# Layer norms applied by ScalarE, and softmax and gamma products held in PSUM, in a four-layer graph network kernel

## The chip, the cores and the metric

The kernel runs on one core of a Trainium2 chip. The metric is the device time of one execution in microseconds (us); the time before is the median of three runs. The engines are called as in the profile: PE (TensorE, matrix products), DVE (VectorE), ACT (ScalarE), POOL (GpSimd) and SP (SyncE, which issues the DMAs). PE reads SBUF and writes PSUM[...].

## The reference, cut to what matters

The input x is 128 graphs of 64 nodes with 512 features, 8192 rows in all. Four layers each end in `x = layernorm(x + layer(x))`.

```python
def _layernorm(x, axis=-1, eps=1e-5):
    m, v = mean(x), var(x)
    return (x - m) / sqrt(v + eps)

x = _layernorm(x + L0(x))     # deg * (x @ Wi.T + b) + adj @ (x @ Wj.T)
x = _layernorm(x + L1(x))     # four attention heads over the 64 nodes, elu, an output head, elu,
                              # feed-forward, and an inner layer norm times gamma plus beta
x = _layernorm(x + L2(x))     # one attention head
x = _layernorm(x + L3(x))     # one attention head
```

An attention is `softmax(where(adj > 0, leaky_relu(f1[:, None] + f2[None, :]), fill))` over 64 neighbours, times the projected rows. Everything is float32.

## The kernel before, in words

The 8192 rows are worked in 32 blocks of two tiles (t = 0, 1) of 128 rows; a tile holds two graphs. A block p goes through stages, each a Python generator: `stage_first` (layer 0), `stage_scores` (attention scores, softmax and aggregation of the four heads), `stage_heads` and `stage_project` (the heads' weights and the output projection), `stage_out` (output head, feed-forward, inner layer norm) and `stage_gat` twice (layers 2 and 3). Large products use seven block products in place of eight (`seven` and `strassen`); their partial sums lie in two PSUM tiles, `stx` and `sty`, which ACT or DVE adds into SBUF piece by piece.

No engine instruction is issued where it is written. `Plan` records each call as a step, and `Plan.order` (line 207) lists the steps by assumed costs (`cost`, line 319), by readiness, by free buffers and by rank; `play` then issues them. So every engine's order comes from the planner, a new step on one engine can shift the order on all of them, and every instruction of the recorded program has line 306 in the profile. `with nc.soon()` lowers the rank of steps by 1000, so that they go ahead of others that are ready. Engines work in order: an instruction that waits holds up all behind it. PSUM is one pool of eight tiles with tag `b`; a step that opens a tile waits until one of the eight is free.

The names that matter below:

- `moments(x, name)`, line 688: `bn_stats` and `bn_aggr` on DVE give mean and variance (`st`, `mv`); two tiny POOL instructions make `rs` = (variance + eps) ** -0.5.
- `normalize(x, name)`, line 699: `moments`, then one DVE instruction over the 128 x 512 tile in SBUF (`x<-x,mv,rs`). It is called for each tile after each of the four layers, 256 times.
- `attention_heads`, line 714: once for each block. PE multiplies `dg` with a block matrix into the PSUM tile `bc`; DVE adds `f` into the SBUF tile `e` (128 x 512: two tiles by four heads by 64 neighbours), then applies the leaky slope, the mask, the maximum, the subtraction; ACT takes the exponential; DVE sums, inverts, and multiplies. PE then transposes `e` into `pt`; ACT copies it to `aT`; `yp` are the products with it.
- `norms(t)` in `stage_out`, line 1053: the inner layer norm. One DVE instruction forms (o - mean) * gamma in SBUF (`o<-o,mv_1i,rows_gamma`), a second multiplies by `rs_1i` and adds x (`x<-o,rs_1i,x`); then `normalize`. 64 times.
- `dots` makes attention scores `f` on DVE (custom instruction, `j<-x,rows`); in the first microseconds the same instruction makes score weights `wa_h` (`j_h`). For blocks 0 and 1, PE makes the scores (`fp`) from transposed rows (`x1Tp`, `x1T`) and `wa_h`.
- For the first four blocks, layer 0 is done plainly: `l` are its products on PE.

Of the kernel before, what the change touches and what calls it, by code (L numbers as in the profile page):

```python
# [12 lines left out]
FP = mybir.dt.float32  # L13
BF = mybir.dt.bfloat16
I32 = mybir.dt.int32
AF = mybir.ActivationFunctionType
ALU = mybir.AluOpType
AX = mybir.AxisListType
PSUM = bass.MemoryType.PSUM

P = 128
# [318 lines left out]
def gnn_stack_kernel(  # L340
# [24 lines left out]
    nc = Plan(tc)  # L365
    NT, D = x.shape
# [13 lines left out]
    small = nc.pool(ctx, name="small", bufs=4)  # L380

    psum = nc.pool(ctx, name="ps", bufs=8, space=PSUM)
# [16 lines left out]
    def rows(srcs, name, tag="rows"):  # L399

        bufs = {"rows": 2, "A": NA}.get(tag, 1)
        t = unit.tile([P, 2, D], FP, tag=tag, bufs=bufs, name=f"rows_{name}")
        for i, src in enumerate(srcs):
            nc.sync.dma_start(out=t[:, i, :], in_=src.partition_broadcast(P))
        return t
# [26 lines left out]
    fill1 = cp.tile([P, 1], FP, tag="fill1", name="fill1")  # L432
# [9 lines left out]
    mask1 = cp.tile([P, N], I32, tag="mask1", name="mask1")  # L442
# [132 lines left out]
    def part_from(name, p, K=D):  # L575

        ring, bufs = RINGS[K]

        def part(q):
            t = unit.tile([P, K // P, D // 2], FP, tag=ring, bufs=bufs, name=f"ws_{name}_{p}_{q}")  # L580
            nc.sync.dma_start(out=t, in_=streams[name][q])
            return t
        return part
# [104 lines left out]
    def moments(x, name):  # L688

        stats = small.tile([P, 6], FP, tag="stats", name=f"st_{name}")  # L690
        mv = small.tile([P, 2], FP, tag="mv", name=f"mv_{name}")
        nc.vector.bn_stats(stats, x)
        nc.vector.bn_aggr(mv, stats)
        rstd = small.tile([P, 1], FP, tag="rstd", name=f"rs_{name}")
        nc.gpsimd.tensor_scalar(rstd, mv[:, 1:2], EPS, None, ALU.add)
        nc.gpsimd.tensor_tensor(rstd, rstd, mhalf, ALU.pow)
        return mv[:, 0:1], rstd

    def normalize(x, name):

        mean, rstd = moments(x, name)
        nc.vector.tensor_scalar(x, x, mean, rstd, ALU.subtract, ALU.mult)

    def dots(f, x, rows, name):

# [8 lines left out]
    def attention_heads(f, name):  # L714

        bc3 = [P, G, N]

        dg = unit.tile([P, G, N], FP, tag="dg", name=f"dg_{name}")
        nc.vector.tensor_tensor(
            dg,  # L720
            f[:, 1, :].unsqueeze(2).to_broadcast(bc3),
            ident2.unsqueeze(1).to_broadcast(bc3),
            ALU.mult,
        )
        yield 2.0
        ps = psum.tile([P, G, N], FP, tag="b", name=f"bc_{name}")
        nc.tensor.matmul(ps, lhsT=bones, rhs=dg, start=True, stop=True)
        e = unit.tile([P, G, N], FP, tag="e", name=f"e_{name}")
        nc.vector.tensor_tensor(e, ps, f[:, 0, :].unsqueeze(2).to_broadcast(bc3), ALU.add)
        nc.vector.scalar_tensor_tensor(e, e, 0.01, e, ALU.mult, ALU.max)  # L730
        nc.vector.copy_predicated(
            e, mask1.unsqueeze(1).to_broadcast(bc3), fill1.unsqueeze(1).to_broadcast(bc3)
        )
        mx = small.tile([P, G], FP, tag="mx", name=f"mx_{name}")
        nc.vector.tensor_reduce(mx, e, AX.X, ALU.max)
        nc.vector.tensor_tensor(e, e, mx.unsqueeze(2).to_broadcast(bc3), ALU.subtract)
        nc.scalar.activation(e, e, AF.Exp)
        sm = small.tile([P, G], FP, tag="sm", name=f"sm_{name}")
        nc.vector.tensor_reduce(sm, e, AX.X, ALU.add)
        r = small.tile([P, G], FP, tag="r", name=f"r_{name}")  # L740
        nc.vector.reciprocal(r, sm)
        nc.vector.tensor_tensor(e, e, r.unsqueeze(2).to_broadcast(bc3), ALU.mult)
        yield 10.0

        pt = psum.tile([P, G // 2, P], FP, tag="b", name=f"pt_{name}")
        with nc.together():
            for q in range(G // 2):
                nc.tensor.transpose(
                    pt[:, q, :], e[:, 2 * q : 2 * q + 2, :].rearrange("p s j -> p (s j)"), ident
                )  # L750
        aT = unit.tile([P, G // 2, 2, N], FP, tag="aTh", name=f"aT_{name}")
        for b in range(2):
            for s in range(2):
                nc.scalar.copy(aT[ts(b, N), :, s, :], pt[ts(s, N), :, ts(b, N)])
        return aT
# [38 lines left out]
    def elu(dst, ps):  # L794

        with nc.soon():
            nc.scalar.activation(dst, ps, AF.Relu, scale=-1.0)
            nc.scalar.activation(dst, dst, AF.Exp, scale=-1.0)
            nc.vector.scalar_tensor_tensor(dst, dst, -1.0, ps, ALU.add, ALU.max)
# [67 lines left out]
    def stage_scores(p):  # L867
# [23 lines left out]
        for h2 in range(H // 2 if p >= 2 else 0):  # L891
            for s in range(2):
# [5 lines left out]
                )  # L898
        yield 3.0
        aT = yield from attention_heads(f, f"1_{p}")  # L900
        yield 3.0

# [93 lines left out]
    def stage_out(p):  # L996

        while p not in outs:
            yield 1.0
        x = xs[p]  # L1000
        who, f = outs.pop(p)
        pt = yield from attention(
            f, 0.01, mask1, fill1.to_broadcast([P, N]), None, f"1o_{p}"
        )
        aT = unit.tile([P, T, N], FP, tag="aT", bufs=2, name=f"aT_1o_{p}")
        with nc.soon():
            for b in range(2):
                for t in range(T):
                    nc.scalar.copy(aT[ts(b, N), t, :], pt[ts(t, N), ts(b, N)])
        yield 2.0  # L1010
        o = unit.tile([P, T, D], FP, tag="o", name=f"o_{p}")
        oT = unit.tile([P, KC, T * P], FP, tag="A", bufs=NA, name=f"oT_{p}")

        ps = [psum.tile([P, D], FP, tag="b", name=f"op_{p}_{t}") for t in range(T)]
        with nc.together():
            for b in range(2):
                for t in range(T):
                    nc.tensor.matmul(
                        ps[t][ts(b, N), :], lhsT=aT[ts(t, N), b, :], rhs=who[ts(t, N), b, :],
                        start=True, stop=True,  # L1020
                    )
        for t in range(T):
            elu(o[:, t, :], ps[t])
        yield 6.0
        b2_sb = rows([b2], f"b2_{p}")[:, 0, :]
        yield 2.0
        for t in range(T):
            ps = psum.tile([P, KC, P], FP, tag="b", name=f"oTp_{p}_{t}")
            with nc.together():
                for k in range(KC):  # L1030
                    nc.tensor.transpose(ps[:, k, :], o[:, t, ts(k, P)], ident)
            nc.scalar.copy(oT[:, :, ts(t, P)], ps)
            nc.gpsimd.tensor_tensor(o[:, t, :], o[:, t, :], b2_sb, ALU.add)
            yield 2.0
        hid = unit.tile([P, 2, T, KC // 2, P], FP, tag="A", bufs=NA, name=f"hid_{p}")
        for q in range(KC // 2):
            ps = psum.tile([P, 2, T * P], FP, tag="b", name=f"hidp_{p}_{q}")
            for c in range(2):
                with nc.together():
                    for k in range(KC):  # L1040
                        nc.tensor.matmul(
                            ps[:, c, :], lhsT=w1_sb[:, k, ts(2 * q + c, P)], rhs=oT[:, k, :],
                            start=(k == 0), stop=(k == KC - 1),
                        )
            for c in range(2):
                nc.scalar.activation(
                    hid[:, q, :, c, :], ps[:, c, :].rearrange("p (t i) -> p t i", t=T), AF.Relu,
                    bias=b1_sb[:, 2 * q + c : 2 * q + c + 1],
                )
            yield 6.0  # L1050
        gamma_sb = rows([gamma], f"gamma_{p}")[:, 0, :]

        def norms(t):
            ot, xt = o[:, t, :], x[:, t, :]
            mean, rstd = moments(ot, f"1i_{p}_{t}")
            nc.vector.scalar_tensor_tensor(ot, ot, mean, gamma_sb, ALU.subtract, ALU.mult)
            nc.vector.scalar_tensor_tensor(xt, ot, rstd, xt, ALU.mult, ALU.add)
            normalize(xt, f"1_{p}_{t}")

        A = lambda k, t: hid[:, k, t, :, :]  # L1060
        nc.gpsimd.tensor_tensor(A(0, 1), A(0, 1), A(1, 1), ALU.add)
        yield from strassen(
            A, part_from("w2", p, D // 2), sums(A, KC // 2, nc.gpsimd), o, KC // 2, f"y_{p}", 1.8,
            whole=norms,
        )
        yield 4.0
# [150 lines left out]
```

## Time and profile before

| | |
|---|---|
| median of 3 runs | 3404.39 us (3404.05 to 3405.88) |
| profiled execution | 3404.41 us |
| its span, first to last instruction | 3402.6 us |
| PE busy | 3285.9 us (97%) |
| DVE busy | 2655.5 us (78%) |
| POOL busy | 1771.1 us (52%) |
| ACT busy | 1163.7 us (34%) |
| mean granted PE clock | 0.989 |

The profiled execution is 1.8 us longer than its span, and lies on the median. A busy PE is one with matrix products in its pipeline. Rows of groups give the engine, the operation, the tiles written and read, shapes and count, then busy time in us and the mean of one in ns, and then the engine's idle time just before them with what ended it. In rows of waits stand the total, the number of times and the longest wait, in us.

### The profile page before, as it was taken

What the parts mean: (1) busy time and instruction counts of PE and PEld (TensorE: products, weight loads), DVE (VectorE), ACT (ScalarE), POOL (GpSimd) and SP (SyncE); (2) the same over time, 40 slices, a digit from 0 to 9 for tenths busy, and PEclk for the clock granted to TensorE, in tenths of its full rate; (3) what the DMA queues carried; (4) which work ended last, traced back from release to release, by engine and by line L of the source; (5) the groups of instructions that cost most, each with busy time, mean ns of one, the idle gap of its engine ahead of it and who ended that gap; (6) DMA issues with size and microseconds to landing.
All of it is one profiled execution on the core that took longest, in us unless ns stands there. A gap on an engine that the chain in (4) does not pass through costs nothing.

```text
span 3402.6 us, 59449 instructions
## 1 busy us (share of the span) xinstructions
PE 3285.9 (97%) x21300; PEld 2898.4 (85%) x21300; DVE 2655.5 (78%) x5696; ACT 1163.7 (34%) x2924; POOL 1771.1 (52%) x1866
## 2 busy tenths in 40 slices
PE   8799999999999999999999999999999999999986
PEld 4688888888888888988888988888988888888874
DVE  7767777888778878778877787878787887877855
ACT  1333333333333333333333333333333333333321
POOL 6854455554455554455554555554555544555432
PEclk9899999999999999999999999999999999999998
DMA  7766666666666666656666666666666676666643
GB/s 279 273 211 204 195 212 220 216 215 221 201 203 220 219 215 220 205 207 220 216 218 215 204 204 221 222 215 219 203 204 219 216 226 207 202 216 211 202 158 118
DMA packets 302500, 720.42 MB, mean 212 GB/s; under 512 B 32848, under 2 KB 42112, under 8 KB 302208
## 3 DMA queue, kind: packets, MB, share of 16 engines
q1 hardware_dynamic: 302208, 716.63, 64.5%
q8 instruction: 171, 2.80, 0.3%
q14 instruction: 121, 0.99, 0.1%
HBM read 683.18 MB, written 33.32 MB: 211 GB/s over the span
## 4 chain that ended last, share of the span: by engine, by line
PE 76%; DVE 16%; DMA 3%; POOL 3%; issue 2%; SPq 1%; ACT 0%; POOLq 0%; DVEq 0%; ACTq 0%
PE stx_h L306 13%; PE stx L306 11%; PE stx_o L306 11%; PE sty_h L306 10%; PE sty L306 9%; PE hidp L306 6%; PE sty_o L306 5%; DVE e L306 4%; PE gp L306 3%; DVE x L306 3%; DVE o L306 2%; PE stx_y L306 1%; PE yp L306 1%; DVE st_1i L306 1%; PE sty_y L306 1%
## 5 line engine op out<-in xcount | busy, mean ns | idle before, releaser
L306 DVE CUSTOM_DVE_ANT_0 j<-x,rows 128x512 bf16<-128x512 f32 x736 | 636.3, 864 | 51.5 <-DMA rows<-d_h 42.5
L306 PE MATMUL stx_h<-ys,wh 128*128 128x128 f32 x3072 | 402.8, 276 | 8.0 <-DVE hT L306 7.9
L306 PEld LDWEIGHTS stx_h<-ys,wh 128*128 128x128 f32 x3072 | 386.2, 192 | 28.0 <-issue 7.3
L306 ACT COPY hT<-stx_h 128x256 f32<-128x256 f32 x384 | 142.5, 372 | 571.9 <-PE stx_h L306 562.7
L306 POOL TENSOR_SCALAR rs<-mv 128x1 f32<-128x1 f32 x256 | 90.9, 355 | 454.2 <-DVE mv L306 449.8
L306 DVE TENSOR_SCALAR x<-x,mv,rs 128x512 f32<-128x512 f32 x256 | 222.0, 867 | 72.4 <-POOL rs L306 72.1
L306 PE MATMUL sty_h<-ys,wh 128*128 128x128 f32 x2048 | 274.0, 277 | 0.0
L306 PEld LDWEIGHTS sty_h<-ys,wh 128*128 128x128 f32 x2048 | 254.3, 192 | 7.1
L306 PE MATMUL sty_o<-ws_wo,hT 128*128 128x256 f32 x1024 | 242.9, 380 | 2.5 <-DMA ws_wo<-d_wo 1.2
L306 PE MATMUL stx_o<-ws_wo_T,s_o 128*128 128x256 f32 x1024 | 244.3, 381 | 0.2
L306 POOL TENSOR_TENSOR ys<-ys,t 128x256 f32<-128x256 f32 x128 | 111.9, 877 | 252.0 <-PE sty_h L306 251.8
L306 DVE TENSOR_TENSOR x<-stx,x 128x256 f32<-128x256 f32 x368 | 154.3, 419 | 112.8 <-PE stx L306 110.3
L306 PE MATMUL hidp<-oT,w 128*128 128x256 f32 x1024 | 234.8, 379 | 0.7 <-ACT oT L306 0.7
L306 ACT ACTIVATE elu<-hT 128x512 f32<-128x512 f32 x256 | 154.1, 602 | 224.8 <-DVE hT L306 220.3
L306 PEld LDWEIGHTS sty_o<-ws_wo,hT 128*128 128x128 f32 x1024 | 189.5, 190 | 28.5 <-POOL hT L306 3.3
L306 PEld LDWEIGHTS hidp<-oT,w 128*128 128x128 f32 x1024 | 191.5, 190 | 25.4 <-ACT oT L306 0.9
L306 PEld LDWEIGHTS stx_o<-ws_wo_T,s_o 128*128 128x128 f32 x1024 | 187.5, 190 | 24.7 <-POOL hT L306 0.3
L306 DVE SCALAR_TENSOR_TENSOR hT<-elu,hT 128x512 f32<-128x512 f32 x256 | 174.9, 684 | 16.3 <-ACT elu L306 14.7
L306 ACT COPY ys<-yp 128x512 f32<-128x512 f32 x256 | 131.2, 606 | 158.3 <-PE yp L306 147.0
L306 DVE BATCH_NORM_STATS2 st<-x 128x6 f32<-128x512 f32 x256 | 176.3, 689 | 4.8
L306 POOL TENSOR_TENSOR rs<-rs,mhalf 128x1 f32<-128x1 f32 x256 | 162.5, 635 | 21.3
L306 DVE TENSOR_TENSOR x<-sty,x 128x256 f32<-128x256 f32 (+1 forms) x184 | 102.1, 555 | 81.6 <-PE sty L306 81.1
(184 smaller groups left out, 7734.8 us busy)
## 6 DMA issues: line engine op xcount, KB each, us to landing
ws_wo_T<-d_wo_T SPq DMA_DIRECT2D x256, 512.0 KB, 3.8
ws_wo<-d_wo SPq DMA_DIRECT2D x192, 512.0 KB, 4.0
ws_W_T<-d_W_T SPq DMA_DIRECT2D x256, 256.0 KB, 3.3
rows<-d_h SPq DMA_DIRECT2D x240, 256.0 KB, 4.5
ws_w_T<-d_w_T SPq DMA_DIRECT2D x112, 512.0 KB, 4.3
ws_W<-d_W SPq DMA_DIRECT2D x192, 256.0 KB, 3.7
ws_w<-d_w SPq DMA_DIRECT2D x84, 512.0 KB, 3.8
ws_w_T<-d_w_T SPq DMA_DIRECT2D x128, 256.0 KB, 4.8
```

The lines of the kernel that those rows point to most:

```text
L306: getattr(getattr(self.tc.nc, s.engine), name)(*map(real, args), **{k: real(v) for k, v in kw.items()})
```

## The change

Three edits. (1) `normalize` now makes `shift` = -mean * rs, a 128 x 1 value, on DVE, and ACT applies the norm to the tile as Identity(rs * x + shift), in place, with both as values for each partition (a token's row). (2) In `attention_heads` the first addition still goes from `bc` to `e`; the leaky step now writes into the PSUM tile `bc`, where mask, maximum, subtraction, exponential and sum then work, and the last multiplication writes `e` from it. (3) In `norms` the product with gamma goes to a new PSUM tile `ng`, and the second instruction reads it from there; both are recorded under `soon()`.

```diff
     def normalize(x, name):
         mean, rstd = moments(x, name)
-        nc.vector.tensor_scalar(x, x, mean, rstd, ALU.subtract, ALU.mult)
+        shift = small.tile([P, 1], FP, tag="shift", name=f"sh_{name}")
+        nc.vector.scalar_tensor_tensor(shift, mean, -1.0, rstd, ALU.mult, ALU.mult)
+        nc.scalar.activation(x, x, AF.Identity, bias=shift, scale=rstd)
...
         nc.vector.tensor_tensor(e, ps, f[:, 0, :].unsqueeze(2).to_broadcast(bc3), ALU.add)
-        nc.vector.scalar_tensor_tensor(e, e, 0.01, e, ALU.mult, ALU.max)
+        nc.vector.scalar_tensor_tensor(ps, e, 0.01, e, ALU.mult, ALU.max)
         nc.vector.copy_predicated(
-            e, mask1.unsqueeze(1).to_broadcast(bc3), fill1.unsqueeze(1).to_broadcast(bc3)
+            ps, mask1.unsqueeze(1).to_broadcast(bc3), fill1.unsqueeze(1).to_broadcast(bc3)
         )
...
-        nc.vector.tensor_reduce(mx, e, AX.X, ALU.max)
-        nc.vector.tensor_tensor(e, e, mx.unsqueeze(2).to_broadcast(bc3), ALU.subtract)
-        nc.scalar.activation(e, e, AF.Exp)
+        nc.vector.tensor_reduce(mx, ps, AX.X, ALU.max)
+        nc.vector.tensor_tensor(ps, ps, mx.unsqueeze(2).to_broadcast(bc3), ALU.subtract)
+        nc.scalar.activation(ps, ps, AF.Exp)
...
-        nc.vector.tensor_reduce(sm, e, AX.X, ALU.add)
+        nc.vector.tensor_reduce(sm, ps, AX.X, ALU.add)
...
-        nc.vector.tensor_tensor(e, e, r.unsqueeze(2).to_broadcast(bc3), ALU.mult)
+        nc.vector.tensor_tensor(e, ps, r.unsqueeze(2).to_broadcast(bc3), ALU.mult)
...
             mean, rstd = moments(ot, f"1i_{p}_{t}")
-            nc.vector.scalar_tensor_tensor(ot, ot, mean, gamma_sb, ALU.subtract, ALU.mult)
-            nc.vector.scalar_tensor_tensor(xt, ot, rstd, xt, ALU.mult, ALU.add)
+            ps = psum.tile([P, D], FP, tag="b", name=f"ng_{p}_{t}")
+            with nc.soon():
+                nc.vector.scalar_tensor_tensor(ps, ot, mean, gamma_sb, ALU.subtract, ALU.mult)
+                nc.vector.scalar_tensor_tensor(xt, ps, rstd, xt, ALU.mult, ALU.add)
             normalize(xt, f"1_{p}_{t}")
```

## The prediction

> **What bounds the kernel now.** First the page's busy line, then PE's waits, then busy time by stretch (PE, PEld, DVE, ACT, POOL, then PE clock, DMA share, GB/s).
>
> ```profile
> PE 3285.9 (97%) x21300; PEld 2898.4 (85%) x21300; DVE 2655.5 (78%) x5696; ACT 1163.7 (34%) x2924; POOL 1771.1 (52%) x1866
> ```
> ```profile
> PE pt L306 <- DVE e L306: 24.4, 13, 10.5
> PE bc L306 <- DVE f L306: 21.3, 7, 4.2
> PE yp L306 <- DVE who L306: 11.1, 12, 1.3
> PE stx_h L306 <- DVE hT L306: 7.9, 4, 5.1
> ...
> PE gp L306 <- ACT aTg L306: 1.5, 2, 0.7
> ```
> ```profile
> 0.00:100.00 100.00, 76.00 (x312) 40.30 (x312) 73.25 (x128) 13.38 (x28) 70.64 (x66) 0.92 0.82 292
> 100.00:200.00 100.00, 90.27 (x689) 84.38 (x690) 65.99 (x112) 39.91 (x90) 71.17 (x49) 0.93 0.79 268
> ...
> 1500.00:1600.00 100.00, 99.86 (x657) 89.07 (x656) 80.92 (x176) 35.35 (x88) 52.80 (x55) 1.00 0.65 214
> ...
> 3300.00:3400.00 100.00, 62.23 (x267) 49.04 (x267) 59.60 (x153) 16.92 (x58) 28.14 (x44) 0.80 0.34 108
> ```
>
> PE bounds it. All that any edit off PE can win is PE's idle time, 3402.6 - 3285.9 = 117 us: 34 us in the first 200, 38 in the last 100, and in 300 to 3100 only some 30 us of waits, of which DVE ends 22 and ACT none. DVE's 78% is not a bound, so its lightening by itself is worth nothing there.
>
> The groups that the change touches, and prices for what it adds, from the groups of DVE (the second fence with shapes kept apart) and of ACT; the figure after the busy time is the mean of one in ns:
>
> ```profile
> L306 DVE TENSOR_SCALAR x<-x,mv,rs 128x512 f32<-128x512 f32 x256 | 222.0, 867 | 72.4 <-POOL rs L306 72.1
> L306 DVE SCALAR_TENSOR_TENSOR x<-o,rs_1i,x 128x512 f32<-128x512 f32 x64 | 84.0, 1313 | 2.8 <-POOL rs_1i L306 2.4
> L306 DVE TENSOR_TENSOR e<-e,mx 128x512 f32<-128x512 f32 x32 | 39.1, 1221 | 1.1
> L306 DVE TENSOR_SCALAR r<-r,has 128x2 f32<-128x2 f32 x64 | 26.1, 409 | 2.2
> L306 DVE TENSOR_TENSOR x<-l,x 128x512 f32<-128x512 f32 x8 | 5.5, 682 | 0.7 <-PE l L306 0.7
> ```
> ```profile
> L306 DVE TENSOR_TENSOR e<-e,r 128x512 f32<-128x512 f32 x32 | 43.1, 1346 | 1.1
> ```
> ```profile
> L306 ACT ACTIVATE e<-e,nm 128x64 f32<-128x64 f32 x128 | 43.0, 339 | 77.9 <-DVE nm L306 77.9
> L306 ACT ACTIVATE e<-e 128x512 f32<-128x512 f32 x32 | 20.2, 633 | 74.1 <-DVE e L306 74.0
> ```
>
> **What the Trainium skill says.** "SBUF — State Buffer", SBUF: two separate sides: DVE's second port pair is GpSimd's too, locked for a whole instruction; a DVE instruction in a two-port mode, or with two SBUF inputs, waits for POOL's. The trace agrees: `x<-x,mv,rs` takes 0.51 us at least, 2.56 at most, 0.87 in the mean; an addition with one input in PSUM (`x<-l,x`) takes 0.68 always. "ScalarE: Activation LUTs", What ACT_TABLE_LOAD costs: 186 ns + 0.833 ns an element, and 93 ns more for each 128 x 1 pointer. The two ACT rows agree: 613 against 633, 332 against 339. A norm with two pointers is then 799 ns, an estimate from that page. "PSUM — Partial Sum Buffer", Summary: evacuate promptly. Following every PSUM tile in the trace from first product to last reader, 4.3 of 8 banks are in use in the mean and never all eight from 300 to 3100 us.
>
> **The change, part by part.**
>
> 1. *256 norms.* DVE loses 256 x 0.867 = 222 us and gains 256 `shift`. Not shown before: at least 0.16 us (the inverse `r<-sm`), at most 0.87 (two SBUF inputs, so it can wait for POOL as its forerunner did); I take 0.38, near `r<-r,has`. DVE -125 us (-181 to 0). ACT gains 256 x 0.80 = 205 us. `shift` still waits for `rs` (72 us); behind it stand, as in the changed program's order, mostly `j` and `x<-stx`, as before. New is that ACT waits for `shift`: behind its 256 norms stand most often copies out of `stx_h`, `yp`, `stx_o`, on which PE waits for its banks.
> 2. *32 softmaxes.* Subtraction and multiplication each have one SBUF input left: 0.69 for 1.22 and 1.35, DVE -38 us. The leaky step keeps two SBUF inputs, and the rest were single-input: at no change, within 0.06 each. The bank is held some 9 us longer a block.
> 3. *64 gamma products.* The second instruction goes from 1.31 to 0.69, -40 us; the first keeps two SBUF inputs. A bank is held 5 us, and the first waits for a free one.
>
> Sum: DVE 2656 - 203 = 2453 us (72%); ACT 1164 + 205 = 1369 (40%). Banks: 32 x 9 + 64 x 5 = 608 us over 3403, 0.2 of a bank; that costs nothing while three stand free. POOL and SP issue what they did; only the stores of x wait for ACT in place of DVE.
>
> What of it reaches PE, by stage:
>
> *Start (0 to 200 us).* DVE's timeline (start, duration):
>
> ```profile
> 91.14 1.43 DVE L306 TENSOR_TENSOR e<-e,mx 128x512 f32<-128x512 f32 x1
> 92.50 1.48 DVE L306 TENSOR_SCALAR x<-x,mv,rs 128x512 f32<-128x512 f32 x1
> 93.90 2.82 DVE L306 CUSTOM_DVE_ANT_0 j<-w,rows_a 128x512 bf16<-128x512 f32 x1
> 96.66 0.67 DVE L306 TENSOR_REDUCE sm<-e 128x8 f32<-128x512 f32 x1
> ```
>
> A norm and a `j` lie between subtraction and sum of the first softmax, while PE waits 10.5 us for `pt`, then 2.9 for the second block's `dg`. In the changed order statistics and that `dg` stand there (0.69 + 0.18 + 0.77 = 1.6 us for 4.2), and the subtraction saves 0.7: `dg`'s wait falls inside `pt`'s. Against it, `fp` moves ahead of the last layer-0 products, at 65 us for PE; its `wa_h` was done at 74.0. The four norms before that took 7.5 us of DVE, so `wa_h` comes at 68 to 71, and PE waits 3 to 6 where it waited 0.6. Net about -4.5. Later the elu steps stand ahead of the `j` that waited 3.8 us for its rows, and that had held PE 5.1 us at 145: half of it, -2.5. Start: -7 (-14 to 0).
>
> *Middle.* DVE is lighter by 203/32 = 6.3 us a block: a third of the 22 us goes, -7. ACT's norms make some copies late: +5. Together -2 (-10 to +12).
>
> *End.* Chains, with no cover. A norm's 0.55 us becomes 0.16 + 0.80 and one more handover of 0.1: +0.5, three times in the last block, +1.5; one product now stands inside the last `pt` wait (4.1 us), -0.5: +1 (-3 to +5).
>
> Sum: 3404.4 - 7 - 2 + 1 = **3396**. The profiled execution and the median are 0.02 us apart, so no correction.
>
> **Rivals.** What a measurement of this kernel tells from no change is 0.2%, 6.8 us.
>
> *Main, faster (0.50):* as above, 3396, alone 3386 to 3397.
>
> *Given back (0.27), 3403.* What the start wins is lost to weights: at 169.9 PE waited 1.2 us for `ws_wo`, whose DMA took 7.7; a PE 7 us earlier waits there. For it: DMA at 0.8 in these windows. Against it: those loads are issued after `f` and `who` of DVE, which come earlier too. The same time results if the change does not do what it says, POOL's lock only moving to `shift` and `j`.
>
> *ACT in PE's way (0.23), slower, 3416.* A norm stands 0.80 us, and 0.28 of waiting for `rs` (72/256), before copies that free PE's banks. It pays for the 8 us won from 8/1.08 = 8 such hits on PE's path, one in four blocks. At 18 hits, with the win kept: 3396 + 19. For it: PE in order, and the planner prices an ACT norm at 0.61. Against it: PE waited for ACT 2.2 us in all, and ACT is idle 60%.
>
> **Numbers.** The range reaches from the start's best end, 3404 - 14 - 10 + 2, to the third case's lower half: 3382 to 3412. Faster 0.50, within 0.2% 0.27, slower 0.23.
>
> **What would show it.** Right: ACT `x<-x,sh,rs` near 0.80 x256, `sh` near 0.38, the three changed DVE rows near 0.69, DVE near 2450 us, PE's busy time as before, `pt` waits under 15 us, PE at 172 or more in the first two stretches (166 now), waits for ACT under 10 us. Wrong: ACT ends 20 us or more of PE's waits, or PE in 300 to 3100 falls below 98.5%; or the start's idle time stays at 34 us.

## The result, and the profile after

The changed kernel takes **3369.36 us** (median of 4 runs, 3365.21 to 3370.87) against 3404.22 us for the kernel before on the same chip: ratio 0.9896, 95% interval 0.9879 to 0.9913. It is faster by 35 us, in the direction of the forecast but outside its range: 3396 was forecast, and 3382 was the lower end. One run of one experiment below, the softmax alone planned anew, took 12081 us and is left out.

The busy line of the page of the changed kernel, and its rows of PE's waits over the whole span:

```profile
PE 3287.4 (98%) x21300; PEld 2901.8 (86%) x21300; DVE 2448.8 (73%) x5696; ACT 1354.8 (40%) x3180; POOL 1719.0 (51%) x1866
```
```profile
PE bc L306 <- DVE f L306: 15.7, 5, 4.6
PE pt L306 <- DVE e L306: 8.4, 5, 3.4
PE bc L306 <- DVE dg L306: 5.8, 2, 5.3
...
PE fp L306 <- DVE wa_h L306: 3.7, 4, 2.4
```

PE works as long as before (3287.4 us for 3285.9) and idles 79.8 us for 116.7. So the 35.4 us of span are all idle time of PE: what it works did not get shorter. Of the waits shown before, the 24.4 us for `pt` are 8.4, and the row of `yp` waiting for `who` (11.1 us) is gone. The groups of the changed kernel that answer to the prices of the forecast, from the rows with shapes kept apart:

```profile
L306 ACT ACTIVATE x<-x,sh,rs 128x512 f32<-128x512 f32 x256 | 207.5, 814 | 201.1 <-DVE sh L306 199.2
L306 DVE SCALAR_TENSOR_TENSOR sh<-mv,rs 128x1 f32<-128x1 f32 x256 | 106.8, 420 | 46.1 <-POOL rs L306 44.8
L306 DVE SCALAR_TENSOR_TENSOR x<-ng,rs_1i,x 128x512 f32<-128x512 f32 x64 | 47.9, 748 | 10.7 <-POOL rs_1i L306 8.6
L306 DVE TENSOR_TENSOR bc<-bc,mx 128x512 f32<-128x512 f32 x32 | 22.3, 698 | 0.9
L306 DVE TENSOR_TENSOR e<-bc,r 128x512 f32<-128x512 f32 x32 | 21.9, 686 | 0.5
```

Each is within 11% of its estimate. The prices were nearly right; what they are worth to PE was not. Where PE's idle time went is seen in the busy time by stretch. First the kernel before, then the changed one (after the length come PE, PEld, DVE, ACT, POOL, PE clock, DMA share and GB/s):

```profile
400.00:3000.00 2600.00, 2574.09 (x16891) 2295.47 (x16890) 2083.95 (x4491) 918.34 (x2300) 1356.16 (x1444) 1.00 0.66 214
```
```profile
0.00:100.00 100.00, 78.74 (x316) 43.28 (x316) 65.78 (x125) 20.37 (x38) 67.82 (x65) 0.93 0.78 277
100.00:200.00 100.00, 90.68 (x687) 84.89 (x686) 68.90 (x118) 38.81 (x88) 72.62 (x50) 0.95 0.80 283
400.00:3000.00 2600.00, 2597.10 (x17125) 2319.32 (x17124) 1932.42 (x4549) 1082.52 (x2539) 1333.00 (x1464) 1.00 0.66 216
```

In the same 2600 us of the middle PE does 234 products more, at 0.152 us each (2597.10/17125) 36 us of work. A second account uses no busy times: the first product of the heads starts at 109.4 us before and 108.4 after; from there to the end of the last such product (32 blocks) it takes 3161.9 and 3126.4; from there to the end 131.3 and 132.3. So up to the heads the start gave 1.0 us, the long part between gave 35.5 (1.1 a block), and the end took 1.0. By PE's idle time, from the traces, the first 300 us gave 5 us (36.8 to 32.1), the last 303 gave 4, and what lies between gave 28 (33.7 to 5.7).

The middle's waits, before and after, in 300 to 3100 us; of each only the costliest rows:

```profile
PE yp L306 <- DVE who L306: 10.5, 11, 1.3
PE sty_y L306 <- DMA ws_w<-d_w: 4.1, 6, 1.2
PE pt L306 <- DVE e L306: 3.9, 8, 0.8
```
```profile
PE sty L306 <- DVE gT L306: 1.1, 1, 1.1
PE sty_y L306 <- DVE x L306: 0.8, 1, 0.8
```

The 31 us of small waits, all rows summed, became 5.5. Eleven of the old ones are the same one: `yp` wants the PSUM tile that DVE's sum into `who` has not yet freed.

### The profile page after: what moved, and what is told of

It reads as the page before. It is cut to its first block, busy times and chain, and to the rows that moved or that the text cites. A ratio compares the mean times of both kernels' runs of the same rounds, so it can differ in the third digit from the quotient of the medians.

```text
span 3367.2 us, 59757 instructions
## 1 busy us (share of the span) xinstructions
PE 3287.4 (98%) x21300; PEld 2901.8 (86%) x21300; DVE 2448.8 (73%) x5696; ACT 1354.8 (40%) x3180; POOL 1719.0 (51%) x1866
## 5 line engine op out<-in xcount | busy, mean ns | idle before, releaser
L306 DVE CUSTOM_DVE_ANT_0 j<-x,rows 128x512 bf16<-128x512 f32 x736 | 616.7, 838 | 67.8 <-ACT x L306 35.7
L306 ACT ACTIVATE x<-x,sh,rs 128x512 f32<-128x512 f32 x256 | 207.5, 814 | 201.1 <-DVE sh L306 199.2
L306 DVE TENSOR_TENSOR hT<-sty_h,hT 128x256 f32<-128x256 f32 x256 | 107.9, 421 | 165.9 <-PE sty_h L306 138.9
L306 POOL TENSOR_TENSOR rs<-rs,mhalf 128x1 f32<-128x1 f32 x256 | 153.8, 601 | 21.3
L306 ACT COPY ys<-yp 128x512 f32<-128x512 f32 x256 | 131.3, 605 | 78.9 <-PE yp L306 73.2
```

Source lines behind the costliest of these rows:

```text
L306: getattr(getattr(self.tc.nc, s.engine), name)(*map(real, args), **{k: real(v) for k, v in kw.items()})
```

## The experiments

All runs were timed in alternation with the kernel before; a difference is against the kernel before of the same runs (its medians: 3403.8 to 3407.3). Theory A at the outset: DVE, lighter by 207 us anywhere, frees PE's banks in time. Rival B: the planner's new order does it. Rival C: the PSUM parts do it.

**How an order is held fixed.** The planner lists the steps of one kernel, and `play` issues others in their places:

```diff
+    def instead(self, *calls):
+        self.steps[-1].emit = list(calls)
...
-                for name, args, kw in s.calls:
-                    getattr(getattr(self.tc.nc, s.engine), name)(
+                calls = [(s.engine, *c) for c in s.calls] if s.emit is None else s.emit
+                for engine, name, args, kw in calls:
+                    getattr(getattr(self.tc.nc, engine), name)(
```

In such kernels the profile's line is 312. "Old order" means that the planner saw the kernel before, "new order" the changed one.

**Order or instructions.** One kernel has the new order with the old instructions, one the old order with the new instructions; the first, for the norm:

```diff
         nc.vector.scalar_tensor_tensor(shift, mean, -1.0, rstd, ALU.mult, ALU.mult)
+        nc.instead()
         nc.scalar.activation(x, x, AF.Identity, bias=shift, scale=rstd)
+        nc.instead(("vector", "tensor_scalar", (x, x, mean, rstd, ALU.subtract, ALU.mult), {}))
```

> The planner sees the changed kernel, so every engine's order of work is the changed kernel's, PE's product for product; but each changed instruction is issued in its old form at that place: the norm as one VectorE operation, the heads' softmax and the gamma product in SBUF. Theory A (the time comes from VectorE's lighter load, which makes its releases of PSUM banks timely): the win goes with the old instructions, 3395 to 3405 us, VectorE busy near 2655 us, PE's waits in 300 to 3100 us back at 25 us or more. Rival B (the time comes from the planner's other order): 3368 to 3380 us, PE's waits in 300 to 3100 us at 10 us or less although VectorE is as busy as before.

> The planner sees the kernel before, so PE's order is the old one; each changed instruction is issued in its new form at the old place (shift on VectorE and norm on ScalarE at the place of the old norm, softmax and gamma product through PSUM). Theory A (lighter VectorE): 3368 to 3380 us, PE's waits in 300 to 3100 us at 10 us or less. Rival B (order): 3395 to 3408 us, PE's waits there still 20 us or more, VectorE busy near 2450.

Measured: new order with old instructions 3382.2 us (ratio 0.9932, 0.9916 to 0.9949), old order with new instructions 3380.0 (0.9928, 0.9913 to 0.9943). The first lies between the two theories' ranges, the second at the edge of A's: each alone brings about two thirds (-22 and -24), and both -35. So the gains don't add. PE's idle time fell by 30 us with the new order and by 24 with the new instructions (37 with both). With the new order and the old instructions its busy time grew by 9 us, at a granted clock of 0.987 where the kernel before had 0.989.

**Parts of the change, planned anew.** Norms alone, and the two PSUM parts alone (edits as in the change's diff):

> Only the norms go to ScalarE; softmax and gamma product as before. VectorE busy 2656 - 222 + 107 = 2541 us. Theory A: the norms take 115 of the 207 us from VectorE, so rather more than half of the win: 3380 to 3388 us. Rival B (order): no tie to VectorE's busy time; anything from 3365 to 3405. Rival C (the PSUM parts bring most of it, as they shorten the chain of the softmax and of the norms themselves): 3394 to 3402.

> Only the two PSUM parts (softmax; gamma product, soon() with it); the norm stays one operation on VectorE. VectorE busy near 2656 - 90 = 2566 us. Theory A: rather less than half of the win, 3385 to 3394 us. Rival B: anything from 3365 to 3405. Rival C: 3368 to 3378.

Measured: norms 3390.6 us (0.9958, 0.9944 to 0.9973), PSUM parts 3384.0 (0.9938, 0.9923 to 0.9953). That is not in proportion to DVE's time: 2487 us busy, 169 less than before, gave 13, and 2504, 151 less, gave 20 (both fell by more than the edits themselves take away). Since the order changes with every part, the next runs keep the old one.

**Old order: norms alone; load put back at the norms; load on ScalarE; another order.** The load after each norm but the first eight is one more DVE instruction, its result unused, in the kernel with all new instructions at the old order; for ScalarE it is three small copies in the changed kernel. The last kernel changes one number of the planner.

```diff
+        return [("vector", "bn_stats", (idle, w1_sb[:, 0, :]), {})]
...
+        return [("scalar", "activation", (idle, w1_sb[:, 0, 0:32], AF.Identity), {})] * 3
...
-WAIT = 0.2
+WAIT = 0.25
```

> The old order; only the norms in the new form. VectorE loses 222 - 107 = 115 of the 207 us. Theory A: the 24 us that the old order wins with all three parts shrink to 55 to 75%: 3386 to 3391 us. Rival D (the PSUM parts carry it): 3396 to 3404 us.

> As the kernel with the old order and the new instructions (3380.0 us), and behind each norm but the first eight VectorE takes the statistics of a constant 128x512 row once more, with its result unused: 248 x 0.69 = 171 us of the 207 that the change took from it. Nothing waits for these but what stands behind them on VectorE. Theory A (at the old order it is VectorE's lateness alone that holds PE): most of the win goes again, 3395 to 3404 us, with waits for VectorE's sums into who and o back. Rival D (the win at the old order is from shorter chains through PSUM or from the lock that VectorE and GpSimd share, not from VectorE's load): 3380 to 3386 us.

> The changed kernel; behind each norm but the first eight ScalarE does three more 128x32 copies of a constant, unused: 248 x 3 x 0.21 = 156 us more on ScalarE (1355 to some 1510 us, 45%), nearly what the norms brought it. The prediction's step (each norm on ScalarE makes copies late, +5 us in the middle, and its third rival's price of 1.08 us a hit): a second such load costs 5 to 20 us, 3374 to 3390. Theory A (ScalarE has slack, its lateness never reaches PE): within 3 us of 3369, and PE's waits for ScalarE in 300 to 3100 us under 5 us.

> The kernel before with one number of the planner changed, the time it allows for a handover (WAIT 0.2 to 0.25): another order, the same instructions. If the better order of the changed kernel is a matter of the planner knowing that VectorE is lighter, this stays within 5 us of 3404. If orders differ by chance that much (rival B'), it moves by 10 us or more in either direction.

Measured: norms at the old order 3413.4 us, **slower** (1.0024, 1.0013 to 1.0034), which no theory had. With the load at the norms' places, 169.9 us of DVE, it is 3386.7 us, a gain of 18.5 where 23.8 stood: the load costs some 5 us, far from theory A's 3395 us or more. The load on ScalarE, 167.6 us, costs nothing (3370.5, ratio 0.9900, 0.9885 to 0.9915). The other WAIT moves 4 us (3401.2), so not every other order wins.

Two timelines of DVE show one way in which the norms lose there. Both kernels have PE's order in common; shown is what DVE does ahead of the sum into `who` from `sty_o` that `yp` waits for. First before, then with the norms alone at the old order (start, duration):

```profile
850.50 0.54 DVE L306 TENSOR_SCALAR x<-x,mv,rs 128x512 f32<-128x512 f32 x1
...
851.29 0.68 DVE L306 CUSTOM_DVE_ANT_0 j<-x,rows 128x512 bf16<-128x512 f32 x1
...
851.90 1.74 DVE L306 SCALAR_TENSOR_TENSOR x<-o,rs_1i,x 128x512 f32<-128x512 f32 x1
853.57 0.41 DVE L306 TENSOR_TENSOR who<-sty_o,who 128x256 f32<-128x256 f32 x1
```
```profile
854.27 0.15 DVE L312 SCALAR_TENSOR_TENSOR sh<-mv,rs 128x1 f32<-128x1 f32 x1
...
855.30 1.56 DVE L312 CUSTOM_DVE_ANT_0 j<-x,rows 128x512 bf16<-128x512 f32 x1 [0.55 <-ACT x L312]
...
856.80 1.74 DVE L312 SCALAR_TENSOR_TENSOR x<-o,rs_1i,x 128x512 f32<-128x512 f32 x1
858.46 0.41 DVE L312 TENSOR_TENSOR who<-sty_o,who 128x256 f32<-128x256 f32 x1
```

Without the norm DVE is 0.4 us shorter (0.15 for 0.54), but the score product `j` behind it now stands waiting for ScalarE's x (0.55) and then takes 1.56 us for 0.68. From the norm's place to the sum, 3.1 us became 4.2. PE's view of the same sum, before and with the norms alone:

```profile
854.03 1.16 PE L306 MATMUL yp<-aT,x 64*128 64x128 f32 x16 [1.32 <-DVE who L306]
```
```profile
858.92 1.16 PE L312 MATMUL yp<-aT,x 64*128 64x128 f32 x16 [2.27 <-DVE who L312]
```

This wait comes in six blocks. Over the middle its total rose, but not by the 8 us that were lost (10.5 before, the row is shown above):

```profile
PE yp L312 <- DVE who L312: 13.6, 6, 2.3
```

PE's idle time over the span rose by only 2.1 us (116.7 to 118.8), its busy time by 7.7 (3285.9 to 3293.6). The granted clock is lower: 0.986 in the median of the eight runs, 0.989 in those of the kernel before. In the profiled run, two of the six waits of 2.27 us are followed by 3.4 us at a clock of 0.50 (from 860.5 and from 2812.9 us); in the kernel before the clock is full from 400 to 3000 us. So a part of the loss is in the granted clock; that the waits bring it down is not shown, and what the rest is stays open.

DVE's waits also say why the load at the norms' places was cheap. With all new instructions at the old order, DVE waited 50.1 us over the span for ScalarE's x at `j`; with the load it waited 8.9. The load filled waits.

**Old order: gamma product alone, and all but it.** In that timeline stands the gamma product's second instruction, 1.74 us, right ahead of the sum. That made theory E: its place is what counts.

```diff
             nc.vector.scalar_tensor_tensor(xt, ot, rstd, xt, ALU.mult, ALU.add)
+            nc.instead(("vector", "scalar_tensor_tensor",
+                        (xt, ps, rstd, xt, ALU.mult, ALU.add), {}))
```

> The old order; only the gamma product goes through PSUM, softmax and norms as before. VectorE loses some 40 us of 207. Theory E (what counts is the place: in the old order the product's second instruction stands on VectorE right before the sum into who whose bank yp waits for, and is 1.7 us long there, 0.7 through PSUM): it brings most of the old order's 24 us, 3380 to 3390 us, PE's waits for who at yp in 300 to 3100 us down from 10.5 to under 5 us. Theory A (VectorE's load, wherever it is taken from): 40 of 207, so about 5 us, 3397 to 3402.

> The old order; norms and softmax in the new form, the gamma product in SBUF as before. VectorE loses 160 of 207 us. Theory E: 3400 to 3415 us, the waits for who at yp in 300 to 3100 us 8 us or more. Theory A: 160 of 207, so 3384 to 3390 us.

Measured: gamma product alone 3407.7 us (1.0003, 0.9995 to 1.0012), all but it 3380.5 (0.9925, 0.9910 to 0.9940). Theory E fell, both ways round, and A's 5 us for the gamma product did not come either. With the gamma product alone PE's waits at `yp` are as long as before, in other places: 17 of 0.6 us for `who`, and 6 (3.4 us in all) for the instruction that reads `ng`. In that kernel the planner did not know of `ng`, so it is not the change's own use of PSUM.

**The softmax alone; and its time put back.** One block's stretch from `bc` to the end of the first 64 `yp` products, before (busy times as above):

```profile
831.02:855.19 24.17, 22.26 (x172) 18.47 (x170) 23.45 (x40) 8.72 (x18) 16.21 (x17) 1.00 0.80 239
```

PE is busy 22.26 us of 24.17, DVE 23.45: 97%, though DVE is busy 78% of the whole. Not every block is like this one. For the 25 blocks whose stretch lies between 400 and 3000 us the trace gives in the mean: length 22.9 us of a block's 102.5, DVE busy 21.5 (94%, and 76% outside the stretch), PE idle 0.93. (The expectation below has DVE at 22.1 and PE at 22.3 us, a miscount: PE is busy 21.96.) Over the 25 blocks PE idles 23.5 us there, of 25.9 in all from 400 to 3000. Eleven blocks hold nearly all of it: six like the one shown, with 1.9 us of idle time each, and five with 1.8 to 2.1 at a DVE share of 93%. Most of the other fourteen have that share too, and PE hardly waits. So the share tells where to look, not whether PE waits. Theory F: DVE's time in this stretch is what holds PE. The softmax lies wholly in the stretch.

```diff
         nc.vector.tensor_tensor(e, e, mxb, ALU.subtract)
-        nc.instead(("vector", "tensor_tensor", (ps, ps, mxb, ALU.subtract), {}))
+        nc.instead(("vector", "tensor_tensor", (ps, ps, mxb, ALU.subtract), {}), load)
...
-        nc.instead(("vector", "tensor_tensor", (e, ps, rb, ALU.mult), {}))
+        nc.instead(("vector", "tensor_tensor", (e, ps, rb, ALU.mult), {}), load)
```

> The old order; only the heads' softmax goes through PSUM. Theory F: in each block VectorE is the bound from bc to the end of yp (in the kernel before it is busy 22.1 of the 22.9 us of this stretch, PE 22.3), and the softmax takes 1.3 us out of just this stretch, once a block: 30 blocks x 0.6 to 1.0 us of PE's idle time, 3378 to 3390 us, VectorE busy 20.5 to 21 us in the stretch. Theory G (the gain of the old order needs the norms and the softmax together; either alone only turns busy time into waiting): 3396 to 3410.

> The old order with norms and softmax in the new form (3380.5 us), and in each heads' softmax VectorE takes the statistics of a constant 128x512 row twice, unused: after the subtraction and after the multiplication, 32 x 2 x 0.69 = 44 us in all, about what the softmax had lost. Theory F (place): the 44 us in this place cost more than the 171 us cost in the norms' places (6.7 us): back to the norms alone, 3400 to 3415. Theory H (what the softmax wins is its shorter chain, or fewer waits for the lock shared with GpSimd, and not VectorE's time in the stretch): 3380 to 3388.

> Only the softmax through PSUM, planned anew (norms and gamma product as before). Theory F: as at the old order, 3378 to 3392 us. Theory G: 3396 to 3406.

Measured: the softmax alone **3370.6 us** at the old order (0.9896, 0.9879 to 0.9912) and 3370.3 planned anew (0.9896, 0.9880 to 0.9913): as much time as the change, and more than F asked. With norms and softmax at the old order, 43.7 us put back in the softmax's place bring 3405.0 (1.0001, 0.9992 to 1.0009): the whole gain of that kernel, 25.7 us, gone. So theory H, that its shorter chain or fewer waits for POOL bring the gain, fell. The same stretch of the same block with the softmax alone at the old order, then with the norms alone:

```profile
826.23:848.14 21.91, 21.91 (x172) 18.56 (x170) 21.19 (x40) 8.58 (x18) 15.89 (x17) 1.00 0.85 246
```
```profile
834.97:860.08 25.11, 22.25 (x172) 18.47 (x170) 23.64 (x39) 10.10 (x19) 15.47 (x17) 1.00 0.81 240
```

With the softmax shorter, PE's 172 products run without a gap, though DVE's share is still 97%. In the mean the stretch fell from 22.9 to 21.8 us. For 32 blocks that makes 35 us (an estimate), the whole gain. Of this, 0.73 us a block are idle time of PE, and 0.34 are busy time for the same products, which the profile now counts as shorter: over the span PE's busy time fell by 8.6 us, at the same granted clock, 0.989. So the softmax alone leaves PE idle 92.4 us, where the changed kernel leaves 79.8. Why the busy time fell is not shown; the profile models the ends of products, and small waits may lie in it. The load made the stretch 0.7 us longer again, and brings back the very wait of the norms alone. The row of waits for `who` at `yp` in 300 to 3100 us, first with the softmax alone, then with the load:

```profile
PE yp L312 <- DVE who L312: 1.2, 3, 0.5
```
```profile
PE yp L312 <- DVE who L312: 14.4, 7, 2.3
```

The planner's order is a second way out of the same stretch: over its 26 blocks in the middle PE idles 7.3 us with the new order and the old instructions, 8.1 with the old order and the new instructions, and 2.1 with both.

**Without the softmax; the gamma product planned anew.**

> The changed kernel without its third part, planned anew: norms on ScalarE and softmax through PSUM, the gamma product in SBUF and without soon(). Theory E: 3380 to 3392 us, as with the norms alone (3390.6). Theory A, or that two parts already bring PE to its floor in the middle: 3368 to 3376 us.

> The changed kernel without its second part, planned anew: norms on ScalarE and the gamma product through PSUM with soon(), the softmax in SBUF as before; VectorE still loses some 165 of the 207 us. Theory F (the softmax's 38 us alone bring the win, as they lie in the stretch that VectorE bounds): 3388 to 3405 us, most of the win lost. Theory A (load in general): 3372 to 3378 us.

> Only the third part, planned anew (with soon()). At the old order it brought nothing (3407.7). Theory F: 3395 to 3408 us. If its planned order with soon() is what matters: 3370 to 3390.

Measured, with all planned results beside each other (differences to the kernel before of the same runs, us):

| part | old order | planned anew |
|---|---|---|
| norms | +8.1 | -13.2 |
| softmax | -33.9 | -34.1 |
| gamma product | +1.5 | -21.3 |
| norms, softmax | -25.7 | -22.2 |
| norms, gamma | not run | -28.1 |
| softmax, gamma | not run | -19.8 |
| all three | -23.8 | -34.9 |

So the softmax is enough, but not needed: norms and gamma product without it still win 28 when planned anew. Theory F's forecasts for this kernel and for the gamma product alone failed (3379.2 and 3386.0 us for 3388 or more): F holds where the order is fixed. The kernel without the gamma product, planned anew, lies in theory E's range (3383.9 us), but E had fallen at the old order. The planned column doesn't follow DVE's load either. Norms added to the softmax lose 12 us, gamma added to it 14, both together lose nothing. A part is seen in the traces: with norms and softmax the time from the last product of the heads to the end is 141.6 us, for 131.4 with the softmax alone; with softmax and gamma PE waits 20.7 us in the middle at `bc` for the scores `f` (17.6 with gamma alone; 3.1 before). Why the planner puts these later was not tried; `soon()` by itself was not run.

**The two ends.** Both kernels start from the changed one; the last line, around `dg`, is in the first of them only.

```diff
+        if name[0] != "0" and int(name.split("_")[1]) == NP - 1:
+            nc.vector.tensor_scalar(x, x, mean, rstd, ALU.subtract, ALU.mult)
+            return
...
-        for s in range(2):
-            for t in range(T):
+        for t in range(T):
+            for s in range(2):
...
+        with nc.soon() if name in ("1_0", "1_1") else ExitStack():
```

> The changed kernel with three edits at its two ends, where PE is idle some 31 us (first 200) and 42 us (from 3200): the last block's norms one operation on VectorE again (0.55 for 0.16 + 0.81 and a handover, three times on the last chain), the scores taken token tile by token tile (one 0.77 us product fewer behind the last norm, in two layers), and dg of the first two blocks put ahead on VectorE (PE waits 5.3 us for the second). From the chain: -0.5 x 3 - 0.8 x 2 = -3 us at the end, 0 to -5 at the start: 3361 to 3367 us. If the new order in the middle is worse, up to 3380: the middle is at PE's floor only as long as the order covers VectorE's work.

> The changed kernel with the last block's norms on VectorE and the scores token tile by token tile, without the third edit of the tail kernel before (dg put ahead), which made the first head product 2 us later: the end 3 to 4 us shorter, the start as in the changed kernel, 3362 to 3366 us.

Measured: 3365.6 us (0.9879, 0.9865 to 0.9894) and 3366.0 (0.9881, 0.9866 to 0.9896). From the last product of the heads to the end it is 128.9 and 127.6 us, for 132.3: the 3 us came in the traces. The first product of the heads came at 110.4 us with `dg` ahead and at 109.4 without, 108.4 in the changed kernel: that edit wins nothing. Both medians are below that of the changed kernel, but the intervals overlap, and the 3 to 4 us were not measured on one chip: that the time falls is not shown.

## Why the prediction was wrong, step by step

- **PE bounds, and only its idle time can be won: right** for the change. Busy +1.5, idle -36.9 us. (With the softmax alone 8.6 us came from PE's busy time.)
- **Prices: right**, the sum for DVE by luck in part. ScalarE's norm was put at 0.80 and took 0.814, `sh` 0.38 and 0.420; DVE 2453 and 2449, ACT 1369 and 1355 us. The second gamma instruction took 0.748, not 0.69. The leaky step, said to change by 0.06 at most, rose from 0.719 to 0.944, 7 us in all. That is the order's doing: at the old order the new form takes 0.77, and with the new order the old form takes 1.06. Instructions that were not touched moved as well, some up, some down (see the last section).
- **"DVE's 78% is not a bound, so its lightening by itself is worth nothing there": the step that failed.** The mean hid a stretch of each block where DVE is busy 94%, and 97% in six of the 25 blocks counted. At a fixed order, time taken from DVE there won 34 us, and time put back there took 26. From this step came the mis-sized term: "a third of the 22 us goes, -7", where of the 31 us of waits all but 5.5 went, 26 us. Waits for DMAs went too (4.8 to 0.8 us), which the term had left out. And it gave the planner's new order nothing in the middle, where with the old instructions this order won 22 us. The place was to be seen: eleven waits at one product, ended by one DVE instruction, at one place of the block. That a busy time of 23.45 in 24.17 us is a bound was shown only by the experiments.
- **"ACT's norms make some copies late, +5": 1.3 us in the changed kernel.** So much PE waits there for ScalarE in 300 to 3100 us, none before. Over the span it is 10.3 us for 2.2, just above the 10 that were to show it right. 168 us more on ScalarE did not matter either. The mechanism exists: at the old order the norms brought waits of `stx_h` for ScalarE's copies (4.4 us in 300 to 3100), and above all DVE waited for ScalarE, which the prediction had named ("behind it stand mostly `j` ..."), but not priced. So the slower rival had a mechanism that exists at the old order, and was wrong of the changed kernel. There DVE waits for ScalarE's x at `j` 27 times (35.7 us) and not 88 times (50.1 us), and PE's waits in the middle are 5.5 us in all.
- **Banks: "costs nothing while three stand free" rests on a count that doesn't decide.** `yp` waited eleven times for the sum that still reads the tile it is to write, with 4.3 of 8 banks in use in the mean; how many were free at these moments was not counted. The longer hold itself cost nothing visible.
- **Start, -7: it gave 1.0** up to the first product of the heads, and 3 us of PE's idle time in the first 200; PE was busy 169.4 us in these two stretches, where 172 was to show it right (166.3 before). The first of its two terms was summed wrongly: 2.6 (4.2 - 1.6), 0.7 and 2.9 us won, and some 3.9 lost at `fp`, make -2.3 and not -4.5. The `pt` wait of 10.5 us and the `stx_h` wait of 5.1 went as said, and `fp` waits 3.7 us, within "3 to 6". But "`dg`'s wait falls inside `pt`'s" failed: PE now stands for the second block's `dg`, as the timeline of PE in the changed kernel shows:

```profile
69.10 2.31 PE L306 MATMUL fp<-wa_h,x1T 128*128 128x8 f32 x10 [2.43 <-DVE wa_h L306]
95.97 2.05 PE L306 MATMUL bc<-dg,bones 128*128 128x512 f32 x2 [5.31 <-DVE dg L306]
```

- **End, +1: right**, +1.0 from the last product of the heads on; and the norm's longer chain there seems real, since taking it back in the last block, together with the scores' order, made the end 3 to 5 us shorter. The two edits were not tried apart.
- **"Given back" to weights: seen and small.** The waits for `ws_wo` came earlier, at 148 and 160 us, 1.7 us each for 1.2 at 169.9.

## What to carry to other kernels

Busy shares are to be read over the stretch that ends in the wait, not over the span: DVE, at 78% of the span, was at 94% in a good fifth of each block, and nearly all of PE's idle time in the middle lay there. An edit that takes 38 us out of this stretch (DVE's busy time fell by 64 in all) won as much time as the whole change. But the share is only a hint: without the waits it was still 97% in the block shown. What shows a bound is to take time out of the stretch and to put it back. Where instructions of two engines are ordered by a planner, a part has to be tried both in the old order and planned anew; their gains overlap, and a move to another engine can turn busy time into a wait for that engine. And PE's busy time and granted clock have to be looked at beside its waits: where the norms alone lost 8 us, PE idled only 2 us more.

## What the runs showed of the hardware

A DVE instruction of 128 x 1 is not always short when it has two SBUF inputs: `sh` takes 0.420 us in the mean, 0.13 at least, and up to 2.3 in the first 100 us, where the norm of 128 x 512 before took 0.51 at its fastest. The Trainium skill's "SBUF — State Buffer", SBUF: two separate sides, says that a DVE instruction with two SBUF inputs is blocked by a POOL instruction that reads SBUF and started first, until that one ends. The trace agrees: of the 256 `sh` in the changed kernel 81 take longer than 0.4 us, and each of these starts while a POOL instruction over a larger tile runs, and ends 0.01 to 0.02 us after it. How small the DVE instruction is doesn't matter then. The trace differs for POOL's own instructions of 128 x 1 that make `rs` and `rs_1i`: 37 of the short `sh` start while one of these runs, and are not held up (0.15 to 0.16 us).

Such times depend on the order: the leaky step of the output head, `e_1o<-e_1o` (128 x 128, unchanged by the edit), took 291 ns in the mean before and 896 ns after, 19 us in all, and the same step of layers 2 and 3 610 and 468. With the old instructions in the new order the first of these takes 895 ns: the order alone did it.
